# Seven front steps of the next image, dealt out ahead of the first slot

## The chip, the cores and the metric

The kernel runs on one core of a Trainium2 chip. The metric is the device time of one execution in microseconds. The median of three runs before the change is 5431.17 us (5421.16 to 5444.6). Beside them there is one execution under the hardware profiler, which took 4810.47 us; every duration in this document is from that execution unless it says otherwise, and its trace counts time from its first instruction.

## What is computed

There are 8 images of 256 channels and 64 x 64 pixels. Each goes through two residual layers, all in float32:

```python
x = x + L0(gn(x))   # 3x3 neighbourhood attention with 4 heads, mixed with
                    # convolution kernels generated per pixel, then a projection
x = x + L1(gn(x))   # modulated deformable 3x3 convolution

# gn: normalization over 32 groups of 8 channels
# L1: om = conv3x3(x, w_off) + b_off       27 channels: 9 x (dy, dx) and 9 masks
#     v[c,k,h,w] = bilinear sample of x at (h,w) + tap k + offset, times sigmoid(mask)
#     out = einsum('bckhw,ock->bohw', v, w)
```

The sampled positions depend on the data, so that layer 1 fetches rows of a table in memory by computed indices.

## The kernel before

**Two streams of work.** For each image there is a *front* and there are *slots*. The front is everything up to the sampling table: layer 0, the second normalization, the table, the offsets and the positions. It is written as a generator (`fronts`, L803, made of `attention`, L586, and `prepare`, L669) that yields 144 times an image; the piece between two yields is a *step*. The slots are the deformable convolution: an image has 8 chunks of 8 rows (512 pixels) and 9 taps, so 72 slots (`SLOTS`, L47). `STEPS` (L53) is 2 x 72 = 144, one step for each half of a slot.

**A slot** has four blocks of 128 pixels. Each block is fetched by one indirect gather on GpSimd (`gather`, L814), which brings four corner rows of 256 floats a pixel into one of 10 buffers of the tag g; ScalarE scales the first corner (`scale`, L828), VectorE adds the other three for two blocks at a time, six instructions (`sum_corners`, L839, L844), and with that the gather buffers are free again. TensorE transposes the four blocks (`transposes`, L858, tile pt), ScalarE copies the result (tile vt, L868), and in the next slot TensorE multiplies it by the tap's weights in two halves m = 0, 1 (`product`, L871, tile po, L890), accumulating over the nine taps. Gathers run up to 18 blocks ahead of the slot, scalings 8, sums 6 (`ahead`, L848).

**The order is written out by hand.** Inside `tc.manual_schedule` (L917) TensorE, ScalarE, VectorE and GpSimd execute in the order in which the code issues. First comes the whole front of image 0, 144 steps. Then ten gathers are issued (L927), and in a loop over i = 0, 2, 4 the first scalings, the first sums and further gathers (L929 to L939). Then the slots run: after each half slot the front is moved on until it has reached

```python
goal = h * STEPS + min(h, STEPS) * STEPS_AHEAD
```

where h counts half slots and `STEPS_AHEAD` is 12. So during image 0's 144 half slots the generator makes 156 steps, and it stays 12 steps ahead of the half slots from then on. In images 1 and later there is one step a half slot.

**The steps that the change touches** are the first of the next image's front: `means` (L184: a small TensorE product gn, L187, and four small VectorE operations, L189 to L193), `ready` (L195: a product gv, L198, a square root on ScalarE with its table load, L200, a reciprocal, L201), `normed` (L233: VectorE writes the first chunk's normalized rows into the tile xn, L248 and L253), a step that is empty in the first chunk, `q` (L299: tile psq, L304, copied by ScalarE, L312), and `k` for its two halves (L345, L331: tile psk, L336, copied by ScalarE, L349). Behind them come the two steps `products` (L361, tile qk, L375, masked by VectorE, L383), `logits` (L389), `generated` with the first part of the softmax (L405, L441), `v`, and so on. Steps 126 to 143 of a front (`prepare`) also issue the table writes (L690) and the loads of the image after (L91) on the SP queue.

Of the kernel before, what the change touches and what calls it, by code (L numbers as in the profile page):

```python
# [51 lines left out]
LEAD = SCALE_AHEAD + GATHERS  # L52
STEPS = 2 * SLOTS  # L53
STEPS_AHEAD = 12


@with_exitstack
def preact_kernel(ctx: ExitStack, tc: tile.TileContext, a: dict, out: bass.AP):
# [95 lines left out]
    for i in range(min(2, B)):  # L154
# [3 lines left out]
        for o in range(H * WP, ENTRIES, P):  # L158
            n = min(P, ENTRIES - o)
# [44 lines left out]
    def folded():  # L204

        ps = psum_a("eff")[:, : NT * HEADS * KK].rearrange(
            "p (c h k) -> p c h k", c=NT, h=HEADS
        )
        for ct in range(NT):
            for h in range(HEADS):  # L210
                for i in range(2):
                    nc.tensor.matmul(
                        ps[:, ct, h, :],
                        w_qkv[h // 2][:, 2 * (h % 2) + i, ct * P : (ct + 1) * P],
                        w_kgT[:, 2 * h + i, :],
                        start=(i == 0),
                        stop=(i == 1),
                    )
        return ps

    def fold(ps):

        for ct in range(NT):
            nc.vector.tensor_scalar(
                w_effT[:, ct, 0 : HEADS * KK],
                ps[:, ct].rearrange("p h k -> p (h k)"),
                alpha,
                None,
                ALU.mult,
            )  # L230
        nc.vector.tensor_scalar(bkg, bkg, alpha, None, ALU.mult)
# [48 lines left out]
    def first_stats(b, c):  # L280
        if c == 0:
            stats0[b] = p2.tile([P, NT, NC, 6], F32, tag="stats0", name=f"stats0_{b}")
        for ct in range(NT):
            nc.vector.bn_stats(
                stats0[b][:, ct, c, :], image[:, ct, c * N : (c + 1) * N]
            )
        if c == NC - 1:
            norm0[b] = Norm(stats0[b], f"0_{b}")
# [514 lines left out]
    def fronts():  # L803
        for b in range(B):
            gn = None
            for got in attention(b):
                gn = got
                yield
            yield from prepare(b, gn)
# [4 lines left out]
    def gather(i):  # L814
        if i >= B * BLOCKS:
            return
        b, n = divmod(i, BLOCKS)
        c, k, j = n // NB // KK, n // NB % KK, n % NB
        g = gp.tile([P, 4 * C], F32, tag="g", name=f"g_{i}")
        nc.gpsimd.indirect_dma_start(  # L820
            out=g,
            out_offset=None,
            in_=tables[b % 2],
            in_offset=bass.IndirectOffsetOnAxis(ap=found[b, c][0][:, j, k : k + 1], axis=1),
        )
        rows[i] = g

    def scale(i):  # L828

        if i >= B * BLOCKS:  # L830
            return
        b, n = divmod(i, BLOCKS)
        c, k, j = n // NB // KK, n // NB % KK, n % NB
        s = gp.tile([P, C], F32, tag="s", name=f"s_{i}", bufs=NB + SUM_AHEAD)
        g, w = rows.pop(i), found[b, c][1][:, j, k]
        nc.scalar.activation(s, g[:, 0:C], AF.Copy, scale=w[:, 0:1])  # L836
        sums[i] = s, g, w

    def sum_corners(i):  # L839

        work = [sums[n] for n in (i, i + 1) if n in sums]
        for q in range(1, 4):
            for s, g, w in work:
                nc.vector.scalar_tensor_tensor(  # L844
                    s, g[:, q * C : (q + 1) * C], w[:, q : q + 1], s, ALU.mult, ALU.add
                )

    def ahead(i):  # L848

        scale(i + SCALE_AHEAD)  # L850
        scale(i + SCALE_AHEAD + 1)
        sum_corners(i + SUM_AHEAD)
        gather(i + LEAD)
        gather(i + LEAD + 1)
# [3 lines left out]
    def transposes(b, n):  # L858
        c, k = divmod(n, KK)
        u = f"{b}_{c}_{k}"  # L860
        pt = [ps_t.tile([P, NB, P], F32, tag="t", name=f"pt_{u}_{ct}") for ct in range(NT)]
        for j in range(NB):
            s = sums.pop(b * BLOCKS + NB * n + j)[0]
            for ct in range(NT):
                nc.tensor.transpose(pt[ct][:, j, :], s[:, ct * P : (ct + 1) * P], ident)  # L865
        v = p2.tile([P, NT, N], F32, tag="vt", name=f"vt_{u}")
        for ct in range(NT):
            nc.scalar.copy(v[:, ct, :], pt[ct].rearrange("p b n -> p (b n)"))  # L868
        state["v", n] = v

    def product(b, n, m):  # L871

        c, k = divmod(n, KK)
        if k == KK // 2 and m == 0:
            r = p1.tile([P, NT, N], F32, tag="r", name=f"r_{b}_{c}")
            if b + 1 < B:
                nc.sync.dma_start(r, kept[b % 2][:, :, c * N : (c + 1) * N])
            state["r"] = r
        if k == 0 and m == 0:

            if b + 1 == B and c % 2:
                state["po"] = [psum_a(f"po_{b}_{c}_{i}") for i in range(NT)]
            else:
                po = ps_o.tile([P, NT, 512], F32, tag="o", name=f"po_{b}_{c}")
                state["po"] = [po[:, i, :] for i in range(NT)]
        po, v = state["po"], state["v", n]
        if m == NT - 1:
            del state["v", n]
        for ct in range(NT):
            nc.tensor.matmul(  # L890
                po[m],
                w_conv[:, ct, k, m * P : (m + 1) * P],
                v[:, ct, :],
                start=(k == 0 and ct == 0),
                stop=(k == KK - 1 and ct == NT - 1),
            )

    def finished(b, c, m):
        if m == 0:
            state["y"] = p1.tile([P, NT, N], F32, tag="y", name=f"y_{b}_{c}")  # L900
        nc.scalar.copy(state["y"][:, m], state["po"][m])  # L901

    def stored(b, c, m=slice(0, NT)):
        r, y = state["r"][:, m], state["y"][:, m]
        x1 = r if b + 1 < B else image[:, m, c * N : (c + 1) * N]
        nc.vector.tensor_add(r, y, x1)
        nc.sync.dma_start(
            out[b].rearrange("(t p) l -> p t l", p=P)[:, m, c * N : (c + 1) * N], r
        )
# [7 lines left out]
    with tc.manual_schedule(engines=ordered):  # L917
        ps = folded()
        for c in (0, 2, 1, 4, 3, 6, 5, 7):
            first_stats(0, c)  # L920
        fold(ps)
        steps = fronts()
        done = 0
        while done < STEPS:
            next(steps, None)
            done += 1
        for i in range(GATHERS):  # L927
            gather(i)
        for i in range(0, SUM_AHEAD, 2):  # L929
            if i == 0:  # L930
                scale(0)
                scale(1)
            scale(i + 2)
            scale(i + 3)
            sum_corners(i)
            gather(i + GATHERS)
            gather(i + GATHERS + 1)
        gather(SUM_AHEAD + GATHERS)
        gather(SUM_AHEAD + GATHERS + 1)  # L939
        last = None  # L940
        for n in range(B * SLOTS + 1):
            late, last = last, None
            if n > 0 and n % KK == 0:
                last = divmod(n // KK - 1, NC)
            for m in range(NT):
                if n < B * SLOTS:
                    if m == 0:
                        transposes(*divmod(n, SLOTS))
                    if not last:
                        ahead(NB * n + 2 * m)  # L950
                if late and m == 0:
                    stored(*late)
                if n > 0:
                    product(*divmod(n - 1, SLOTS), m)
                if last:

                    finished(*last, m)
                    ahead(NB * n + 2 * m)
                    if n == B * SLOTS:
                        stored(*last, slice(m, m + 1))  # L960

                h = NT * n + m + 1
                goal = h * STEPS + min(h, STEPS) * STEPS_AHEAD
                while (done - STEPS) * STEPS < goal:
                    next(steps, None)
                    done += 1

# [78 lines left out]
```

## Time and profile before

| | |
|---|---|
| median of the three runs | 5431.17 us |
| the profiled execution | 4810.47 us |
| its span, first to last instruction | 4808.7 us |
| mean granted TensorE clock | 0.985 |
| busy share: TensorE, VectorE, GpSimd, ScalarE | 96%, 87%, 61%, 51% |
| front of image 0 alone | 0 to about 312 us |
| first gather issued | 312.66 us |
| first deformable product (po) | 333.62 us |
| first finished chunk stored | 409.72 us |
| from there to the same chunk of image 1 | 594.4 us |
| the same stretch in the five images after | 576.4 to 579.7 us |

A row of the profile is a group of instructions: the line of the kernel, the engine, the operation, and out<-in by the names of tiles. PE is TensorE's matmul and PEld its weight load, DVE is VectorE, ACT ScalarE, POOL GpSimd, SP the queue that issues plain DMAs. In answers in order of time the first two numbers are the start and the duration in microseconds, and a bracket at the end holds the idle time before and what ended it. The profile counts a float32 matmul as two instructions, so that the four matmuls of q are eight rows.

### The profile page before, as it was taken

To read this page: it belongs to the slowest core of one execution; us is meant where nothing else is said; L and a number is where in the kernel's file an instruction comes from. 1 tells how busy PE (TensorE), PEld (TensorE's weight loads), DVE (VectorE), ACT (ScalarE), POOL (GpSimd) and SP (SyncE) were. 2 spreads that over 40 slices of the span, in tenths; PEclk is the share of its full clock that TensorE was granted. 3 is DMA by queue.
4 is the path that set the end of the run, shared out by engine and by line. 5 is a ranking of instruction groups with operands and counts; after the bars stand their busy time and mean duration, and the time that the engine had idled before them with its cause. 6 is when DMAs were issued, how large, how long until landed. Compare 5 with 4: busy or idle time off the path is not lost.

```text
span 4808.7 us, 80080 instructions
## 1 busy us (share of the span) xinstructions
PE 4597.8 (96%) x26848; PEld 2612.5 (54%) x26848; DVE 4185.7 (87%) x10066; ACT 2464.7 (51%) x5312; POOL 2954.5 (61%) x2310
## 2 busy tenths in 40 slices
PE   8979999999999999999999999999999999998888
PEld 5635555555545555455555555555555555544343
DVE  5568988899988998988988899899998899988887
ACT  3335555455555555555554555555555555554554
POOL 0026666566656666466674666756666666657776
PEclk9989999999999999999999999999999999999999
DMA  2077878888898878988889888888788888888998
GB/s 98 23 243 280 285 281 329 292 306 305 295 338 308 296 287 288 354 292 294 309 298 332 303 293 295 317 330 293 288 299 335 297 293 302 285 307 336 365 370 319
DMA packets 472649, 1414.24 MB, mean 294 GB/s; under 512 B 46814, under 2 KB 114654, under 8 KB 472108
## 3 DMA queue, kind: packets, MB, share of 16 engines
q0 software_dynamic: 331776, 1208.11, 68.6%
q1 hardware_dynamic: 138444, 197.65, 11.5%
q8 instruction: 211, 3.46, 0.3%
q10 hardware_dynamic: 2016, 3.38, 0.2%
q14 instruction: 202, 1.65, 0.1%
HBM read 1276.02 MB, written 132.94 MB: 293 GB/s over the span
## 4 chain that ended last, share of the span: by engine, by line
PE 73%; DVE 12%; DMA 10%; issue 3%; ACT 2%; POOL 0%; DVEq 0%; POOLq 0%; ACTq 0%
PE po L890 29%; DMA g<-table,idx 9%; PE pt L865 8%; DVE s L844 7%; PE om L701 6%; PE psk L336 4%; PE psq L304 4%; PE psv L336 4%; PE proj L561 3%; PE av L549 3%; PE qk L375 2%; PE vk L531 2%; PE ptab L681 2%; PE gt L427 1%; PE gen L409 1%
## 5 line engine op out<-in xcount | busy, mean ns | idle before, releaser
L820 POOL DMA_INDIRECT g<-table,idx x2304 | 2952.0, 1281 | 1832.8 <-DVE s L844 784.7
L844 DVE SCALAR_TENSOR_TENSOR s<-g,wt,s 128x256 f32<-128x256 f32 x6912 | 2814.0, 477 | 207.2 <-ACT s L836 197.7
L890 PE MATMUL po<-vt,w_conv 128*128 128x512 f32 x4608 | 2203.6, 604 | 31.4 <-ACT y L901 31.4
L836 ACT ACTIVATE s<-g,wt 128x256 f32<-128x256 f32 x2304 | 1090.3, 511 | 613.5 <-DMA g<-table,idx 514.0
L890 PEld LDWEIGHTS po<-vt,w_conv 128*128 128x128 f32 x4608 | 816.9, 193 | 762.1 <-issue 703.8
L868 ACT COPY vt<-pt 128x512 f32<-128x512 f32 x1152 | 616.7, 588 | 350.8 <-PE pt L865 349.4
L865 PE MATMUL pt<-ident,s 128*128 128x128 f32 x4608 | 661.2, 282 | 71.0 <-DVE s L844 52.0
L865 PEld LDWEIGHTS pt<-ident,s 128*128 128x128 f32 x4608 | 530.6, 143 | 324.8 <-issue 135.5
L701 PE MATMUL om<-xn,w_off 128*32 128x512 f32 x2304 | 288.1, 596 | 0.0
L383 DVE TENSOR_TENSOR qk<-qk,near_k 128x400 f32<-128x400 f32 x256 | 134.0, 568 | 161.9 <-PE qk L375 158.7
L336 PE MATMUL psv<-xn,w_qkvT 128*128 128x264 f32 (+1 forms) x1088 | 258.9, 382 | 0.0
L336 PE MATMUL psk<-xn,w_qkvT 128*128 128x264 f32 (+1 forms) x1088 | 254.6, 379 | 0.0
L336 PEld LDWEIGHTS psv<-xn,w_qkvT 128*128 128x128 f32 x1088 | 201.2, 191 | 85.2 <-issue 49.5
L336 PEld LDWEIGHTS psk<-xn,w_qkvT 128*128 128x128 f32 x1088 | 201.7, 190 | 83.0 <-issue 38.8
L304 PE MATMUL psq<-xn,w_qkvT 128*128 128x512 f32 x512 | 236.2, 603 | 10.1 <-DVE wk L516 8.6
L561 PE MATMUL proj<-acc,w_projT 128*128 128x512 f32 x512 | 240.7, 593 | 0.7 <-ACT acc L556 0.7
L710 ACT ACTIVATE om<-om,b_off 128x512 f32<-128x512 f32 x64 | 44.1, 688 | 270.3 <-PE om L701 270.3
L701 PEld LDWEIGHTS om<-xn,w_off 128*32 128x32 f32 x2304 | 74.2, 109 | 199.2 <-issue 161.0
L349 ACT COPY k<-psk 128x264 f32<-128x264 f32 (+1 forms) x272 | 100.2, 372 | 157.0 <-PE psk L336 155.4
L358 ACT COPY v<-psv 128x320 f32<-128x320 f32 (+1 forms) x272 | 106.2, 414 | 138.6 <-PE psv L336 138.0
L253 DVE TENSOR_SCALAR xn<-x,gn 128x576 f32<-128x576 f32 (+2 forms) x256 | 177.2, 734 | 0.0
L304 PEld LDWEIGHTS psq<-xn,w_qkvT 128*128 128x128 f32 x512 | 95.2, 190 | 143.3 <-issue 91.1
(94 smaller groups left out, 3430.3 us busy)
## 6 DMA issues: line engine op xcount, KB each, us to landing
table<-ts SPq DMA_DIRECT2D x384, 176.0 KB
g<-table,idx POOLq DMA_INDIRECT x2304
out_dram<-r SPq DMA_DIRECT2D x63, 512.0 KB
x<-in_x_dram SPq DMA_DIRECT2D x61, 512.0 KB
x<-x SPq DMA_DIRECT2D x56, 512.0 KB
r<-x SPq DMA_DIRECT2D x56, 512.0 KB
w_conv<-in_w_conv_dram SPq DMA_DIRECT2D x1, 2304.0 KB
x<-in_x_dram ACTq DMA_DIRECT2D x3, 512.0 KB
```

Of the source, the lines that this page charges most:

```text
L253: nc.vector.tensor_scalar(xn[:, ct, o : o + hi - lo, 1 : W + 1], xt[:, ct, lo * W : hi * W].rearrange("p (r w) -> p r w", w=W), gn[:, 0, c ...
L304: nc.tensor.matmul(ps, w_qkvT[:, ct, m * P : (m + 1) * P], window(self.xn, ct, 4), start=(ct == 0), stop=(ct == NT - 1),)
L336: nc.tensor.matmul(ps[:, : (hi - lo) * WP], w_qkvT[:, ct, o : o + P], self.xn[:, ct, lo:hi, :], start=(ct == 0), stop=(ct == NT - 1),)
L549: nc.tensor.matmul(av[64 * h : 64 * h + 64, g, t * T * T : (t + 1) * T * T], self.vk[:, t, o : o + 64], self.wk[2 * g + h][:, i * n + t * ...
L561: nc.tensor.matmul(ps, w_projT[:, ct, m * P : (m + 1) * P], self.acc[:, ct].rearrange("p (t y x) -> p y t x", y=T, x=T), start=(ct == 0), ...
L701: nc.tensor.matmul(ps[32 * g : 32 * g + 32, :], w_off[:, ct, k, :], window(xn, ct, k), start=(n < 4), stop=(n >= KK * NT - 4),)
L820: nc.gpsimd.indirect_dma_start(out=g, out_offset=None, in_=tables[b % 2], in_offset=bass.IndirectOffsetOnAxis(ap=found[b, c][0][:, j, k : ...
L836: nc.scalar.activation(s, g[:, 0:C], AF.Copy, scale=w[:, 0:1])
L844: nc.vector.scalar_tensor_tensor(s, g[:, q * C : (q + 1) * C], w[:, q : q + 1], s, ALU.mult, ALU.add)
L865: nc.tensor.transpose(pt[ct][:, j, :], s[:, ct * P : (ct + 1) * P], ident)
L868: nc.scalar.copy(v[:, ct, :], pt[ct].rearrange("p b n -> p (b n)"))
L890: nc.tensor.matmul(po[m], w_conv[:, ct, k, m * P : (m + 1) * P], v[:, ct, :], start=(k == 0 and ct == 0), stop=(k == KK - 1 and ct == NT - 1),
```

## The change

After image 0's 144 front steps three more steps are made (means, ready, normed of image 1) before the first gather is issued. In the loop that issues the first scalings and sums, two steps are made behind the first pair of sums (the empty one and q) and one behind each of the two others (the halves of k). `done` starts at 151, and the remaining five steps ahead are spread over the 144 half slots of image 0. From the end of image 0's slots on, the order is that of before.

```diff
 STEPS_AHEAD = 12
+STEPS_FIRST = 7
...
         steps = fronts()
-        done = 0
-        while done < STEPS:
+        for n in range(STEPS):
             next(steps, None)
-            done += 1
+
+        for n in range(STEPS_FIRST - 4):
+            next(steps, None)
         for i in range(GATHERS):
             gather(i)
         for i in range(0, SUM_AHEAD, 2):
...
             sum_corners(i)
             gather(i + GATHERS)
             gather(i + GATHERS + 1)
+            for n in range(2 if i == 0 else 1):
+                next(steps, None)
+        done = STEPS + STEPS_FIRST
...
                 h = NT * n + m + 1
-                goal = h * STEPS + min(h, STEPS) * STEPS_AHEAD
-                while (done - STEPS) * STEPS < goal:
+                goal = h * STEPS + min(h, STEPS) * (STEPS_AHEAD - STEPS_FIRST)
+                while (done - STEPS - STEPS_FIRST) * STEPS < goal:
                     next(steps, None)
                     done += 1
```

On TensorE this puts gn, gv, the products of q and of k in front of slot 0's transposes, where before they stood between slots 0 and 3. On VectorE the four small operations, the reciprocal and the normalizing stand in front of the first sums. On ScalarE the table load and the square root stand in front of the first scaling, the copies of q between the scalings of blocks 3 and 4, and the copies of k between those of 5 and 6 and behind that of 7.

## Prediction

> **What bounds the kernel now.** I read the page's forty slices first, then the waits of TensorE, then a table by stage around the first slot, and last the instructions there in order of time. The slices say that TensorE is the busy engine from the third slice on, and that the one hole is early:
>
> ```profile
> PE   8979999999999999999999999999999999998888
> PEclk9989999999999999999999999999999999999999
> DMA  2077878888898878988889888888788888888998
> ```
>
> Each slice is 120 us. The weak ones, the third of both upper rows, hold the change from the first image's front to its first slot. The waits between 290 and 420 us say what TensorE lacked there:
>
> ```profile
> PE pt L865 <- DVE s L844: 12.5, 2, 10.9
> PE gv L198 <- DVE gnd L193: 4.9, 1, 4.9
> ACT s L836 <- DMA g<-table,idx: 21.3, 18, 4.9
> ```
>
> Columns: total us, times, longest. TensorE waits for the corner sums of the first samples, these for ScalarE's scaling, and that for the gathers. In stretches (wall us, then busy us of PE, PEld, DVE, ACT, POOL, then granted clock, DMA share, GB/s):
>
> ```profile
> 304.00:312.00 8.00, 6.77 (x56) 3.14 (x54) 3.83 (x15) 2.64 (x6) 0.00 (x0) 1.00 0.53 170
> 312.00:316.00 4.00, 0.00 (x0) 0.00 (x0) 3.65 (x15) 0.00 (x0) 2.73 (x3) 0.74 0.37 124
> 316.00:320.00 4.00, 0.00 (x0) 0.00 (x0) 1.04 (x4) 0.51 (x1) 3.07 (x4) 0.50 0.81 247
> 332.00:336.00 4.00, 4.00 (x12) 2.63 (x12) 3.29 (x10) 2.94 (x7) 3.09 (x4) 0.50 1.03 407
> 336.00:340.00 4.00, 4.00 (x8) 1.62 (x7) 4.00 (x11) 1.51 (x3) 2.19 (x3) 0.77 1.02 408
> 344.00:409.00 65.00, 61.76 (x397) 37.49 (x395) 52.37 (x124) 34.85 (x79) 44.22 (x34) 1.00 0.71 253
> ```
>
> So there is a gap of some 22 us (311.6 to 333.6) with 5 us of TensorE work in it, and behind it the clock is half until about 337.7. From 344 on TensorE is 95% busy, VectorE 81%: TensorE binds. The rows that the change touches:
>
> ```profile
> 322.55 1.12 PE L865 MATMUL pt<-ident,s 128*128 128x128 f32 x4 [10.93 <-DVE s L844]
> 331.46 0.56 PE L198 MATMUL gv<-gnd,gmat 128*128 128x2 f32 x2 [4.93 <-DVE gnd L193]
> 333.62 5.70 PE L890 MATMUL po<-vt,w_conv 128*128 128x512 f32 x8
> 339.15 3.61 PE L304 MATMUL psq<-xn,w_qkvT 128*128 128x512 f32 x8
> 331.12 1.28 ACT L200 ACT_TABLE_LOAD   x1
> 335.30 1.51 DVE L253 TENSOR_SCALAR xn<-x,gn 128x576 f32<-128x576 f32 x2
> ```
>
> **What moves, and its price.** The seven steps are the next image's means, its deviation, its first normalized rows, an empty step, q, and both halves of k. They hold no DMA; nothing of them goes through SP or POOL, and the ten first gathers keep their order. None is removed: afterwards 149 steps instead of 156 are dealt to the first image's 144 half slots, and from its end on the order is as before. Only that image can gain or lose. Its later steps come up to seven half slots earlier, fading to none; those that store, load or write tables go through SP earlier by as much, each an issue of 0.4 to 0.6 us on a queue with time between its issues, so I cost them at nothing (if a table write met the full DMA of 770 to 861 us, at most its own few us).
>
> TensorE: q 3.44, k 2.68 and 1.78 us by the chain of waits at full clock, together 7.9, and two tiny products (0.42 and 0.56). VectorE: four small operations over 0.74 us (330.57 to 331.31), a reciprocal 0.17, zeroing and normalizing 1.6; 2.5 in all. ScalarE: square root 0.26 with its table load, two q copies of 0.59, k copies of 2 x 0.27 and 4 x 0.38: 3.2 without the load. Today all this stands inside slots 0 to 3, where TensorE's part is on the path.
>
> **The gap walked through.** The statistics are ready at 316.55. Each hop of the chain gn, four small operations, gv, square root, reciprocal is taken from today's rows (0.15 us from VectorE to TensorE, 0.39 from TensorE to the others): gn ends 317.1, gv 318.95, the reciprocal 319.8, the normalized rows 321.55. The first scaling now waits behind the square root in ScalarE's queue until 319.6 (it ran at 316.82), but the second could not run before 320.28 anyway, so the pair is done at 320.8. The first six sums start at 321.55 behind the normalizing and end at 324.0 instead of 322.9. The buffer that this frees is asked for by the eleventh gather, which POOL's own pace of 1.25 us brings at 325.47: no cost.
>
> q starts at 321.7, cold: a pass of 128x512 takes 0.853 us (5.70 us row, weight loads spaced 0.34 + 0.52), warm 0.43. Both ends: 6.8 us if it stays cold throughout, 3.4 if warm. Today the first full-sized products start at 333.6 and the clock is released some 4.1 us later; I take that row, so five passes are cold and q ends at 327.2. The Trainium skill (TensorE: Matmul & The Clock Gate, Part 1) puts it as a window: about 3.4 us idle halves the clock, about 3.4 us of steady work frees it. It speaks against filling a gap with matmuls that all run at half speed. With 3.4 us q would end at 326.8. The granted clock of 0.50 agrees that the array is cold here, but today's four cold passes of the convolution (some 2 us lost) disappear in exchange, since q and k warm the array first; so the rule costs nothing on balance, by either number.
>
> k follows without a hole: first half to 329.9, second to 331.7. ScalarE copies q at 325.5 and 327.6, so the scalings of blocks 4 and 5 come at 328.2 to 329.2 (today 324.2 and 325.5), those of 6 and 7 behind the k copies, done at 331.6. That is the new wait: queued behind these copies are the scalings, and VectorE's sums wait for those. Sums of blocks 6 and 7 end near 334.0 (today 330.6). Slot 0's transposes run at 331.7 to 332.6 instead of 322.5; they cost nothing, because slot 0's product waits behind slot 1's transposes. Steps 8 and 9 (the qk products, 0.9 each) then fill TensorE to 334.4, slot 1's transposes end at 335.3, and the first convolution product starts at 335.3 against 333.6.
>
> Beyond that VectorE is short: qk masks 2.1 and the logits 3.0 us now come before the sums that slot 2 needs, so its transposes start near 344, about 1.4 us after TensorE is free; I find one more such wait, 1.8 us, ahead of slot 4, behind the softmax twists (2.8 us). Counting on with 0.87 us for a slot's transposes and 3.44 for its products, TensorE has finished slot 4's product and the next chunk's q near 372.5. Today the same step ends with slot 7's product at 393.7. The three products between (5, 6 and 7 with their transposes) are 3 x 4.31 = 12.9 us, so the new kernel stands there at 385.4: **8 us ahead**.
>
> A second way to the same number: from the first stored chunk to that of the next image took 594.4 us in image 0 (409.72 to 1004.17), and 576.4 to 579.7 in the five after it. That stretch has 63 slots of image 0 and 9 of the next, so 10.5 of the 12 extra steps: 16.8 us over the mean of 577.6, or 1.6 a step. Seven steps less are 11.2, minus the 1.7 of the late first product: 9.5, and less the 3 us of waits for VectorE 6. I take 8.
>
> The profiled execution took 4810.5 us (span 4808.7); the median of the runs shown is 5431.2, 12.9% more, and no row tells why. I take the gap to stretch likewise: 8 x 1.129 = 9 us, 5422. All runs shown lie within 23 us, and 0.5% of the time, 27 us, is about what a measurement can tell from no change; this gain is below that.
>
> **The rivals.**
> *Absorbed.* The gathers begin at the same 312.66, and DMA shares run at 1.03 around 332 and 0.98 at 770 to 861 (the table writes). If a timed run is held by gathers rather than by TensorE, work taken off TensorE brings nothing: 5431. For it speaks that scaling waits 21.3 us for gathers in the window; against it that TensorE is 98 to 100% busy in each 100 us from 400 to 700. Chance 0.13.
> *All of image 0's excess goes.* The first chunk took 76.1 us from the first product (333.6 to 409.7) against 68.3 in the next image, 7.8 more; with the 16.8 that is 24.6, times 1.129 28: 5403, just over 0.5% faster. It needs the remaining five steps to be free as well, in waits that the profile doesn't show. Chance 0.17.
> *VectorE stays behind.* Slots start with fewer sums in hand than today. VectorE is 91% busy between 400 and 500 us, so the debt may not be repaid: a wait of some 1.5 us ahead of each slot's transposes, over three chunks (27 slots), is 40 us, minus the 11.2 taken off: +29, times 1.129 +33: 5464. It decides from the seventh such slot on (7 x 1.6 = 11.2). Against it: before, VectorE idled 1.2 to 3.7 us at a time between 344 and 355, which is what repays the debt. Chance 0.14.
>
> **How the numbers follow.** Likeliest, 0.56: 5422, with its own range of 5408 to 5438 (cold or warm q, 3 us; no or twice the VectorE waits, 3 us; the runs' own spread, some 10 us). Range for 8 in 10: 5400 to 5450, which takes in the absorbed case, the edge of the second rival and half of the way to the third. Faster by over 0.5% is the second rival, 0.17; slower the third, 0.14; within, 0.69.
>
> **What would show it.** Right: q and k rows of image 1 between 321 and 332 us, the first passes at 0.85; the first product near 335; the wait of pt for the sums no longer 10.9 us but two or three of 1 to 2; the first stored chunk about 8 us earlier; later images unchanged at 577. Wrong: waits of pt for s spread over the first chunks (VectorE), longer waits of the scalings for gathers with TensorE idle (absorbed), or later images whose time changed, which nothing here foresees.

## The result and the profile after

| | before | after |
|---|---|---|
| median | 5431.17 us (5421.16 to 5455.17, 9 runs) | 5441.59 us (5398.45 to 5461.17, 9 runs) |
| ratio after / before | | 1.0011, 95% interval 0.9991 to 1.0031 |
| profiled execution, span | 4810.47, 4808.7 us | 5435.43, 5433.7 us |

No difference that this comparison can tell. Two later comparisons of the same two kernels gave 1.0012 (0.9995 to 1.0029) and 1.0020 (1.0006 to 1.0034). Weighting the three by the inverse square of their half widths gives 1.0015 with a half width of 0.001: the changed kernel is some 8 us slower, where 9 us less was forecast. Neither of the first two alone tells that from no change.

One thing has to be known before any number here is compared. The runs went to several chips, and **the chips differ by 13%, each of them in every execution**: on one (the quick chip below) every execution of every kernel took 4791 to 4833 us, on the others 5393 to 5508. The profiled execution shown with the kernel before was of the first kind, the timed runs beside it of the second. So the profile of after can't be laid beside that of before to tell what the change did; each is compared with a profile of its own kind below.

The slices of after, for those shown of before:

```profile
PE   8988999999999999999999999999999999997777
PEclk9999999999999999999999999999999999998888
DMA  2177679777797677877788777877679776788876
```

The slices are longer now (136 us), and the weak third one is still weak. In the same columns as before (wall, busy us of PE, PEld, DVE, ACT, POOL, clock, DMA share, GB/s), the stretches around the first slot:

```profile
316.00:320.00 4.00, 1.52 (x4) 1.00 (x4) 2.75 (x9) 1.22 (x4) 2.86 (x4) 0.50 0.98 303
332.00:336.00 4.00, 1.50 (x9) 0.65 (x10) 0.00 (x0) 1.01 (x2) 3.09 (x4) 1.00 0.95 366
336.00:340.00 4.00, 2.41 (x21) 1.91 (x21) 1.57 (x4) 0.00 (x0) 0.49 (x1) 0.54 1.03 418
```

The gap of 316 to 320 has TensorE work now, as meant. But from 332 to 340, where before was full (4.00 and 4.00), TensorE is busy for 3.9 of 8 us and VectorE for 1.6 and ScalarE for 1.0. The waits of TensorE from 290 to 420 us:

```profile
PE qk L377 <- issue: 7.1, 13, 1.2
PE gn L189 <- DVE mv L184: 5.3, 1, 5.3
```

The waits of pt for the sums (12.5 us) are gone. In their place stand 13 short ones of qk for "issue", in which TensorE waited for nothing that the profile shows. In order of time:

```profile
319.11 5.46 PE L306 MATMUL psq<-xn,w_qkvT 128*128 128x512 f32 x8 [1.55 <-issue]
324.41 4.62 PE L338 MATMUL psk<-xn,w_qkvT 128*128 128x132 f32 x24
328.87 1.04 PE L867 MATMUL pt<-ident,s 128*128 128x128 f32 x8
329.83 1.08 PE L377 MATMUL qk<-k,q 64*64 64x100 f32 x36
331.20 0.37 PE L377 MATMUL qk<-k,q 64*64 64x100 f32 x2 [0.28 <-issue]
332.62 0.33 PE L377 MATMUL qk<-k,q 64*64 64x100 f32 x3 [1.05 <-issue]
333.34 0.24 PE L377 MATMUL qk<-k,q 64*64 64x100 f32 x1 [0.39 <-issue]
...
338.32 0.95 PE L377 MATMUL qk<-k,q 64*64 64x100 f32 x13 [0.23 <-issue]
339.21 1.97 PE L867 MATMUL pt<-ident,s 128*128 128x128 f32 x8
340.97 2.99 PE L892 MATMUL po<-vt,w_conv 128*128 128x512 f32 x4
```

The first 36 of 64 qk rows take 1.08 us, the other 28 take 8 us: they come in ones, twos and threes, and the starts lie 0.71 us or twice that apart. The first product waits for their end.

### The profile page after: what moved, and what is told of

Same layout as the page of the kernel before. It is cut to its first block, busy times and chain, and to the rows that moved or that the text cites. A ratio compares the mean times of both kernels' runs of the same rounds, so it can differ in the third digit from the quotient of the medians.

```text
span 5433.7 us, 80082 instructions
## 1 busy us (share of the span) xinstructions
PE 4892.5 (90%) x26848; PEld 2766.8 (51%) x26848; DVE 4187.6 (77%) x10066; ACT 2454.4 (45%) x5312; POOL 2984.2 (55%) x2310
## 5 line engine op out<-in xcount | busy, mean ns | idle before, releaser
L892 PE MATMUL po<-vt,w_conv 128*128 128x512 f32 x4608 | 2308.4, 629 | 34.0 <-ACT y L903 14.0
L838 ACT ACTIVATE s<-g,wt 128x256 f32<-128x256 f32 x2304 | 1063.8, 510 | 458.2 <-DMA g<-table,idx 400.7
L892 PEld LDWEIGHTS po<-vt,w_conv 128*128 128x128 f32 x4608 | 853.0, 201 | 810.5 <-issue 761.4
L377 PE MATMUL qk<-k,q 64*64 64x100 f32 x4096 | 224.6, 267 | 200.8 <-issue 191.1
L377 PEld LDWEIGHTS qk<-k,q 64*64 64x64 f32 x4096 | 143.3, 138 | 336.3 <-issue 298.3
L306 PE MATMUL psq<-xn,w_qkvT 128*128 128x512 f32 x512 | 239.5, 610 | 23.1 <-DVE wk L518 20.0
L551 PE MATMUL av<-wk,vk 100*64 100x64 f32 x4096 | 200.5, 258 | 33.8 <-issue 32.3
L551 PEld LDWEIGHTS av<-wk,vk 100*64 100x64 f32 x4096 | 173.7, 168 | 109.3 <-issue 89.9
L558 ACT COPY acc<-av 128x512 f32<-128x512 f32 x128 | 75.1, 587 | 306.5 <-PE av L551 231.7
L538 ACT COPY vk<-vk 100x512 f32<-100x512 f32 x256 | 138.2, 590 | 154.4 <-PE vk L533 145.7
```

Source lines behind the costliest of these rows:

```text
L306: nc.tensor.matmul(ps, w_qkvT[:, ct, m * P : (m + 1) * P], window(self.xn, ct, 4), start=(ct == 0), stop=(ct == NT - 1),)
L377: nc.tensor.matmul(both[h][64 * t : 64 * t + 64, n : n + NK], self.qt[r, ct, o * T * T : (o + 1) * T * T], kt[r, ct, :, T * o : T * o + KT ...
L551: nc.tensor.matmul(av[64 * h : 64 * h + 64, g, t * T * T : (t + 1) * T * T], self.vk[:, t, o : o + 64], self.wk[2 * g + h][:, i * n + t * ...
L892: nc.tensor.matmul(po[m], w_conv[:, ct, k, m * P : (m + 1) * P], v[:, ct, :], start=(k == 0 and ct == 0), stop=(k == KK - 1 and ct == NT - 1),
```

## The experiments

Marks below are us after the start of the last group of omt products (four, the last of the offsets) of image 0's front (310.54 in the profile of before), since the fronts differ by a few us from execution to execution.

### Both kernels on the quick chip

The two kernels as they are, a profile of each, on the chip where the kernel before took 4816.5 us (35 runs, 4804.68 to 4830.69).

Before:

> The kernel of before once more, to have its profile beside that of the changed kernel under like conditions (the first profile of before was 12.9% shorter than the runs, that of after was not). Theory 1 (the timed executions of both kernels lose time in stretches in which TensorE issues the small qk and av products slowly, and the first profile of before happened not to): span near 5430 us, granted clock near 0.94, some 300 us of PEld qk waiting for issue, and the first stored chunk at about 425 plus the 8 us that were forecast, so 433. Rival (the slow issue came with the change): span near 4810 us and almost no such wait.

After:

> The changed kernel once more: whether its profile repeats. Theory 1: 5430 to 5450 us, first product near 341 us, first stored chunk near 425. Rival (two states that any execution may fall in): now and then 4800 us, with the first product near 334.

4830.46 us before, 4823.97 after, both within the spread of before alone, so the totals tell nothing and the traces have to. Both expectations of about 5430 us were missed because the executions fell on the quick chip; neither trace has the slow issue, so they don't decide between the theories on it. From image 0's front to the first stored chunk of image 1, the kernel before in one row of the stretches (columns as above):

```profile
313.00:1009.00 696.00, 660.22 (x3906) 382.32 (x3907) 613.71 (x1480) 361.93 (x786) 449.87 (x343) 0.98 0.83 296
```

and the changed kernel:

```profile
313.00:1000.00 687.00, 660.49 (x3906) 380.56 (x3907) 613.92 (x1480) 360.50 (x787) 449.16 (x343) 0.99 0.84 300
```

The same 3906 matmul rows, the busy time of TensorE and VectorE the same within 0.3 us and of the others within 2 us, and 9 us less wall: what is saved in these two traces is TensorE's idle time and nothing else. By the marks the ninth chunk is stored at 686.8 us, against 693.6 and 696.4 in the two profiles of before: 6.8 to 9.6 us. The gap itself, changed kernel:

```profile
323.63 5.78 PE L306 MATMUL psq<-xn,w_qkvT 128*128 128x512 f32 x8 [1.55 <-DVE xn L255]
329.25 4.62 PE L338 MATMUL psk<-xn,w_qkvT 128*128 128x132 f32 x24
333.71 1.04 PE L867 MATMUL pt<-ident,s 128*128 128x128 f32 x8
334.67 1.63 PE L377 MATMUL qk<-k,q 64*64 64x100 f32 x64
336.24 1.09 PE L867 MATMUL pt<-ident,s 128*128 128x128 f32 x8
337.17 1.88 PE L892 MATMUL po<-vt,w_conv 128*128 128x512 f32 x4
```

Here the 64 qk rows take 1.63 us in one piece, and the first product starts 23.6 us after the mark's zero. TensorE's waits from 316 to 420 us, before:

```profile
PE pt L865 <- DVE s L844: 12.1, 2, 10.5
PE gv L198 <- DVE gnd L193: 5.0, 1, 5.0
```

and after:

```profile
PE gn L189 <- DVE mv L184: 5.4, 1, 5.4
PE qk L377 <- ACT k L351: 2.5, 1, 2.5
...
PE pt L867 <- DVE s L846: 0.9, 1, 0.9
```

### Three steps, and nine, on the same chip

*Three*: only means, ready and normed come ahead of the gathers; this was meant to give TensorE nothing large in the gap. *Nine*: both qk steps come ahead as well.

```diff
# three
-STEPS_FIRST = 7
+STEPS_FIRST = 3
-        for n in range(STEPS_FIRST - 4):
+        for n in range(STEPS_FIRST):
-            for n in range(2 if i == 0 else 1):
-                next(steps, None)
# nine
-STEPS_FIRST = 7
+STEPS_FIRST = 9
-        for n in range(STEPS_FIRST - 4):
+        for n in range(3):
-            for n in range(2 if i == 0 else 1):
+            for n in range(2 if i == 0 else 1 if i == 2 else 3):
```

Three:

> Only the three normalization steps (means, ready, normed) come ahead of the gathers; q and k stay in the slots. Theory of the forecast (what is moved into the gap is worth its TensorE time): 1 to 3 us of gain, since these steps hold 1 us of TensorE and one wait of 4.9 us that already lay in the gap; first product 2 to 4 us earlier than before's. Rival (the gain of the moved steps is eaten by slow issue of the first qk products, which seven steps push into the gap): three steps leave qk in the slots as before, and the first product comes near 331 us instead of 341.

Nine:

> Nine steps ahead: the two qk steps also stand before slot 0. Theory of the forecast: TensorE has 1.8 us less in the slots, total 10 us under before, first product no later than with seven. Rival (slow issue of qk): the first transposes wait behind qk, first product near 341 us as with seven or a few us later, total within 3 us of before.

Three: 4812.64 us (13 runs), ratio 0.9998 (0.9984 to 1.0012). Nine: 4810.43 (22 runs), ratio 0.9983 (0.9973 to 0.9994), 8 us faster by the ratio, 6 by the medians, where 10 had been expected. Their ninth chunks stand at 689.5 and 689.9. So bringing steps forward pays on this chip; for three steps the mark says 4 to 7 us and the totals say no difference, which is as far as one trace and an interval of 13 us go. The changed kernel with its seven steps was timed here only by its one profiled execution: its own gain there rests on the trace.

*Three* is not the contrast that it was meant to be. With the normalized rows ready, the steps dealt to the first two half slots are q and the first half of k, and these ran in the gap all the same, ahead of the first product:

```profile
330.57 6.15 PE L306 MATMUL psq<-xn,w_qkvT 128*128 128x512 f32 x8
336.56 2.84 PE L338 MATMUL psk<-xn,w_qkvT 128*128 128x132 f32 x16
```

So the two runs don't tell what q and k in the gap are worth from what the earlier normalization is worth. The first product came at 25.4 with three and 27.6 with nine, later than with before (22.7 and 23.1), where an earlier one, and one no later than with seven, had been expected. A later first product alone is thus no sign of a loss: it counts whatever ran ahead of it.

### The same on a slower chip, with the seven in one lump, and with twelve

Another chip; before takes 5431.88 us (51 runs). *Lump* makes all seven steps before the first gather. *Twelve* makes all twelve, the last six behind the third pair of sums.

```diff
# lump
-        for n in range(STEPS_FIRST - 4):
+        for n in range(STEPS_FIRST):
-            for n in range(2 if i == 0 else 1):
-                next(steps, None)
# twelve
-STEPS_FIRST = 7
+STEPS_FIRST = 12
-        for n in range(STEPS_FIRST - 4):
+        for n in range(3):
-            for n in range(2 if i == 0 else 1):
+            for n in range(2 if i == 0 else 1 if i == 2 else 6):
```

After:

> The changed kernel, timed again. Theory 1 (the forecast's mechanism: TensorE work moved into the gap is taken off the slots): where executions take about 4815 us, 6 to 10 us less than before, ratio 0.998 to 0.9985; in the trace, from the last omt product of image 0's front to the first stored chunk of image 1 some 687 us against 695. Theory 2 (nothing is gained, the sums and the gathers set the pace): ratio 1.000, the same stretch within 3 us of before. If executions take about 5430 us, theory 1 still has 8 us less in that stretch.

Before:

> Before, for the trace on this chip. Both theories: from the last omt product of image 0's front to the first stored chunk of image 1 694 to 697 us if executions take about 4815 us; about 785 us if they take 5430 (778.8 was seen for the changed kernel there; theory 1 adds 8).

Lump:

> All seven steps ahead of the first scalings and sums, not dealt out between them. ScalarE's scalings wait behind all copies of q and k, the first sums come some 9 us later, and the gathers wait for their buffers. Theory 1: first convolution product 31 to 33 us after the last omt product instead of 23.6, so 7 to 9 us of the gain gone, total within 2 us of before. Theory 2 (it does not matter where they stand, the slots catch up): like the changed kernel.

Twelve:

> All twelve steps ahead of the first slot (the two qk steps, the logits, gen and the first part of v behind the third pair of sums). Theory 1: TensorE's moved work grows from 7.9 to 13.5 us, of which the gap still hides what fits before the sums of slot 1 are ready; 9 to 12 us under before, at most 3 better than seven. Theory 2: 0. The rival that VectorE stays behind: first product 29 us or later after the last omt product, and total no better than before.

| | median us | ratio (95%) |
|---|---|---|
| before, its profiled execution | 5427.12 | |
| after | 5438.20 | 1.0012 (0.9995 to 1.0029) |
| lump | 5448.72 | 1.0032 (1.0020 to 1.0045) |
| twelve | 5429.56 | 0.9998 (0.9982 to 1.0014) |

None gains here, whatever the number of steps, and the lump is slower than before. It puts q and k ahead of the first gathers and so the sums behind them, and the waits of pt that the change removes are back in its trace:

```profile
332.68 0.83 PE L867 MATMUL pt<-ident,s 128*128 128x128 f32 x4 [2.98 <-DVE s L846]
335.06 1.11 PE L867 MATMUL pt<-ident,s 128*128 128x128 f32 x4 [1.54 <-DVE s L846]
```

That is 4.5 us. The lump's median is 10.5 us behind the changed kernel's, but the two intervals overlap, and its first product (30.9) and ninth chunk (785.5) stand within 1.5 us of the changed kernel's, so the trace shows no more than the waits. In *twelve* the first product came at 37.4, the first chunk at 122.4 and the ninth at 772.6. A first product after 29 and no gain were to be the signs of VectorE staying behind, but TensorE's waits for the sums are 1.7 us there up to 435 us. What the chips do differently stands in the waits of the whole execution. The changed kernel on this chip:

```profile
PE qk L377 <- issue: 184.1, 262, 2.7
PE pt L867 <- ACT vt L870: 95.1, 24, 10.0
```

and on the quick one, where this is TensorE's longest entry and qk never waits for issue:

```profile
PE pt L867 <- DVE s L846: 39.2, 61, 7.1
```

The marks of stored chunks (us after the zero):

| kernel, chip | first po | chunk 1 | 3 | 5 | 7 | 9 |
|---|---|---|---|---|---|---|
| before (profile shown), quick kind | 23.1 | 99.2 | 242.8 | 389.7 | 550.7 | 693.6 |
| before, quick | 22.7 | 98.2 | 243.5 | 390.3 | 551.6 | 696.4 |
| after, quick | 23.6 | 100.8 | 240.4 | 383.9 | 547.0 | 686.8 |
| before, slower | 22.9 | 109.1 | 272.1 | 447.4 | 613.3 | 768.5 |
| after, same slower chip | 31.6 | 117.8 | 288.0 | 453.5 | 628.6 | 784.2 |
| after (first profile), slower kind | 31.8 | 116.1 | 284.3 | 450.1 | 624.8 | 778.8 |

On the slower chip the changed kernel is 8.7 us late already at the first product and the first chunk, and 10 to 16 us at the ninth. Adding up the wall time of all bursts of the small products qk and av (first start to last end) from the zero to the ninth chunk gives some 40 us for either kernel on the quick chip, and on the slower one 91 (before) and 108 (after): about 17 us more slow issue in image 0 of the changed kernel, which is more than the gain. For before 785 us had been expected at the ninth chunk, and it stood at 768.5. The later images are alike in both kernels, 576 to 582 us on the quick chip and 647 to 659 on the slower. How far one trace can be trusted shows behind the ninth chunk, where the order of the two kernels is the same: there the changed kernel's profile is 14 us the shorter one (spans 5431.4 and 5425.3, less the marks and the zeros of 313.40 and 308.88). What repeats is the late first product, 31.6, 31.8 and 32.2 in three profiles of the changed kernel, where the same order has 23.6 on the quick chip.

### Is it the length of a run of small products?

In the slow bursts above, TensorE ran fast for the first tens of small matmul rows and then slowly. One theory: a long unbroken run of them is what falls behind. The changed kernel puts the two qk steps back to back (64 rows), where before a half of po stood between (32 and 32). *Split* is the changed kernel with the first half slots' steps held back so that a half of po stands between the two qk steps. *Spread* is the kernel before with a group of 32 av rows moved one step on, out of the step that holds 32 qk rows.

```diff
# split (changed kernel)
+                held = {1: 1, 2: 1, 3: 2, 4: 3, 5: 5, 6: 6}.get(h)
                 while (done - STEPS - STEPS_FIRST) * STEPS < goal:
+                    if held is not None and done - STEPS - STEPS_FIRST >= held:
+                        break
# spread (kernel before)
             a_.products(1)
-            if d:
-                d.weighted(0)
             yield None
             a_.logits()
             if d:
+                d.weighted(0)
```

Split:

> The changed kernel with its two first qk steps kept apart: the second is held back until half of a convolution product stands between them, and the steps after it catch up by the seventh half slot. Theory A (where executions take 5430 us, TensorE's small matmuls are supplied slowly once more than some 80 of them with as many weight loads follow each other; the change brought the first two qk steps together, 64 matmuls in 8.8 us instead of 2 x 0.93, and that took the gain away): the first product stands at 23 to 25 us after the last omt product instead of 31.6, both qk steps at 0.93, and the time is 8 us under the changed kernel's, so 5430 against before's 5432, or less. Where executions take 4815 us: like the changed kernel, within 3 us. Theory B (the slow supply depends on the traffic of the gathers, not on the run of small matmuls): qk stays slow, some 8 us, wherever it stands among the first gathers.

Spread:

> Before, with one step changed in every chunk: the first half of the attention product (32 av matmuls) goes from the step of the second qk products to the next one, so that nowhere 64 small matmuls stand together. Theory A: where executions take 5430 us, the bursts of 64 that took 4 to 12 us there and 2.0 where they take 4815 are gone, 56 of them: 250 to 500 us less, 4930 to 5180. Where executions take 4815: within 10 us of before. Theory B: no more than 30 us less.

Before took 5480.4 us (35 runs) on this chip. Split 5482.66, ratio 1.0002 (0.9985 to 1.0019); spread 5479.22, ratio 0.9996 (0.9977 to 1.0015). The theory falls: spread was to take 250 to 500 us less. In spread a single qk step of 32 rows, with half a slot's product ahead of it, still breaks up:

```profile
480.91 0.60 PE L375 MATMUL qk<-k,q 64*64 64x100 f32 x12
481.83 0.24 PE L375 MATMUL qk<-k,q 64*64 64x100 f32 x1 [0.32 <-issue]
482.55 0.40 PE L375 MATMUL qk<-k,q 64*64 64x100 f32 x3 [0.47 <-issue]
484.01 0.33 PE L375 MATMUL qk<-k,q 64*64 64x100 f32 x3 [1.05 <-issue]
```

And in split the first two qk steps take 1.61 and 0.93 us, but now the k copies of ScalarE ahead of them come late, so that the first po comes at 29.8 us and not at 23.6:

```profile
336.81 0.38 ACT L351 COPY k<-psk 128x264 f32<-128x264 f32 x1 [4.03 <-PE pt L867]
339.68 0.38 ACT L351 COPY k<-psk 128x264 f32<-128x264 f32 x1 [2.49 <-remote]
```

This looks like a stall that has moved to ScalarE. It has not. A copy waits for a semaphore, a counter that the engine before it raises, and the trace keeps the times of these updates. Both copies start 0.02 us after an update (336.79 and 339.66) of the one semaphore that only TensorE's matmuls raise, while the two groups of psk that they copy had ended at 332.06 and 332.95 by the trace. So TensorE's signals were 4.7 and 6.7 us late, and 2.87 us apart, four times 0.72. Since the ends of matmuls are modelled in these profiles, this does not tell whether the products themselves or only their signals were late. "remote" stands where no instruction was found to have ended shortly before the update: all 158 such waits of ScalarE and VectorE in the first profile of after, and all 157 in that of split, are for this semaphore of TensorE.

The other theory on record, that the traffic of the gathers makes the qk products slow wherever they stand among the first gathers, does not fit split's qk of 1.61 and 0.93 us either; what it says of late signals was not tested.

### Warming TensorE's clock in the gap

The changed kernel with five unread products put between the last offset product and the normalization steps; the rest as it is.

```diff
+        warm = psum_a("warm")
+        for n in range(5):
+            nc.tensor.matmul(
+                warm, w_qkvT[:, 0, 0:P], window(xn2[1], 0, 4), start=(n == 0), stop=(n == 4)
+            )
         for n in range(STEPS_FIRST - 4):
             next(steps, None)
```

After:

> The changed kernel as it is, timed once more. On a chip where the kernel before takes about 4815 us the theory (TensorE gets the 7 to 10 us that the first image's excess loses, and nothing takes them back) gives 4807, a ratio of 0.9980 to 0.9985, with the ninth chunk stored some 687 us after the last offset product of the first front (693.6 and 696.4 before). On a chip where it takes about 5430 us the theory of slow issue (the products issue slowly from the first chunk on, which takes the gain back) gives a ratio of about 1.001, the first deformable product 31 to 32 us after that point and the ninth chunk near 780. The rival, that the change is absorbed everywhere, gives 1.000 on either chip.

Warm:

> The changed kernel with five unread 128x512 products (4.3 us cold) put on TensorE between the last offset product and the three normalization steps, so that its clock may be released when q comes. The prediction's theory, that the cold clock costs nothing on balance, since slot 1's sums are last and not TensorE: q takes 3.6 to 4.9 us instead of 5.8, k ends up to 2 us earlier, the first deformable product comes within 1 us of the changed kernel's, and the total is within 3 us of it. The rival, that the cold products in the gap are paid for in full: first product 2 us earlier and total 2 us less on a 4815 us chip. If the clock counts only what runs without a pause, the five products end before q starts and nothing changes: q stays at 5.8.

A slower chip again (before 5472.58 us, 43 runs). After: 5478.63 us, ratio 1.0020 (1.0006 to 1.0034). Warm: 5483.59, ratio 1.0020 (1.0004 to 1.0037). The first interval leaves out 1.000, if narrowly: here the change costs time, and is not merely absorbed. A ratio of about 1.001, a first product at 31 to 32 and a ninth chunk near 780 had been expected of slow issue; 1.0020, 32.2 and 783.5 came. In warm:

```profile
315.72 4.55 PE L930 MATMUL warm<-xn,w_qkvT 128*128 128x512 f32 x10
321.20 0.35 PE L189 MATMUL gn<-mv,gmat 128*128 128x2 f32 x2 [0.93 <-DVE mv L184]
...
324.40 5.37 PE L306 MATMUL psq<-xn,w_qkvT 128*128 128x512 f32 x8 [1.55 <-DVE xn L250]
329.61 4.62 PE L338 MATMUL psk<-xn,w_qkvT 128*128 128x132 f32 x24
334.06 1.04 PE L867 MATMUL pt<-ident,s 128*128 128x128 f32 x8
341.55 2.94 PE L377 MATMUL qk<-k,q 64*64 64x100 f32 x64 [6.45 <-ACT k L351]
```

The five products ran warm (0.91 us each, clock 1.00 from 312 to 324), not cold as I had put it. But they end at 320.27, q starts at 324.40, and in the 4.1 us between stand only the two tiny products. Then q takes 5.37 us against 5.68 in after. The granted clock by stretches:

```profile
320.00:324.00 4.00, 0.99 (x5) 0.59 (x4) 2.52 (x10) 0.66 (x2) 3.08 (x4) 1.00 0.82 269
324.00:328.00 4.00, 3.60 (x6) 1.68 (x7) 3.80 (x9) 1.41 (x3) 3.08 (x4) 0.70 0.95 343
328.00:332.00 4.00, 4.00 (x18) 2.73 (x17) 3.24 (x8) 2.31 (x7) 3.08 (x4) 0.88 1.02 414
```

At half speed for 0.30 / 0.5 x 4 = 2.4 us of the second stretch and 1.0 of the third, the clock was half from about 325.6 to 329.0: it still was full when q began and fell while q ran, 5.3 us after the five products. This is nearly the third case of the expectation. So whether a warm q would bring the 2 us was not settled. The late signals of TensorE are here as well: qk runs in one piece, ScalarE's k copies come 6.4 us late ("remote", again TensorE's semaphore), and the first po comes at 31.3 us against 32.2 in after.

## Why the prediction was right and wrong

**The total: in range, by luck.** 5441.6 us lies within the 5400 to 5450 that were given, and a difference too small to tell was given 0.69. But it lies outside the likeliest case's own range (5408 to 5438), and what held it there is not in the forecast: a gain of 7 to 10 us that the quick chip's trace shows, and, if that gain is there on the slower chips too, some 16 us lost again; a stall of TensorE that the forecast did not know is the likely place.

**Where the gap is and what fills it: right.** On the quick chip the wait for the first sums went from 12.1 to 0.9 us and the one for the normalization chain from 5.0 to 0.9, and the wait for the statistics (gn, 5.4 us) came in front, where nothing else is to do.

**The walk through the gap: right within 1.2 us.** Counted from the zero, q was forecast at 11.2 and came at 10.05, 5.5 us long and measured 5.78 (five to six of eight passes cold); the first product was forecast at 24.8 and came at 23.6. For slots 2 and 4, 1.4 and 1.8 us of waiting for VectorE's sums were forecast; one wait of 0.9 came. "VectorE stays behind" did not happen on either kind of chip. Two slips of the working cost nothing: the cold row of 5.70 us holds about five cold passes ((5.70 - 3.44) / 0.42) and not the four set against them, and the five later images average 577.9 us and not 577.6.

**The cold clock costs nothing on balance: not settled.** In the one run that was to warm q, the clock fell while q ran.

**"8 us ahead": right in size at the end of image 0 on the quick chip, wrong in place.** I compared the same front step at two different slots (4 and 7) and took off three products, as if no step went with slots 5 to 7. Compared at the same slot, the changed kernel still makes 149/144 steps a half slot, and after 9 slots (18 half slots) it has been spared only 18 x 7/144 = 0.9 steps, 1.4 us at the 1.6 us a step of the second way, which the late first product takes back. The first chunk was 1.6 to 2.6 us later, where I had written "about 8 us earlier" as the sign of being right; the lead grew over the image (chunk 5: 5.8 to 6.4, chunk 9: 6.8 to 9.6). The second way, steps times 1.6 less the late product, has a mechanism that fits the growing lead: 9.5 forecast.

**"I take the gap to stretch likewise": the step that failed.** The 12.9% between the profiled execution and the timed runs was no stretch. It is the difference between two chips, and in image 0 most of it is one thing: bursts of small products that issue slowly. There they grew from 40 to 91 us in the kernel before, 51 of the 72 us by which that stretch is longer (768.5 against 696.4); in the whole execution, 337 of 597 us. A stretched gap would have given 9 us. Instead the qk products that the change brings forward met slow issue before the first product, and lost 8 us there, where before ran them fast:

```profile
352.24 0.93 PE L375 MATMUL qk<-k,q 64*64 64x100 f32 x32
355.02 0.94 PE L375 MATMUL qk<-k,q 64*64 64x100 f32 x32
```

That before is spared at this place does not hold for every execution: in spread, which has the same order up to here, the first qk step broke up too (29 rows in 1.18 us, then three single ones) and took 4.0 us. The total came out at 1.0015 instead of 0.9984: the sign was wrong on the chips that were timed. 5422 was forecast and 5441.6 came; against the before of the same comparison that is 10 us more instead of 9 less. That the stall ahead of the first product makes up this difference is likely, by the 8 us and by its return in three profiles, but no run takes the stall away and leaves the change: split and warm kept it in another form.

**The rivals.** *Absorbed* is the nearest by number on the slower chips, but not by its mechanism: the scalings' waits for gathers are shorter there (390 to 443 us in the whole execution against 550 on the quick chip), and TensorE waits more. *All of image 0's excess goes* fell: image 0 took 586.0 us on the quick chip, still above the 576 to 582 of the others, and twelve steps gained nothing in total where they ran.

**What stays open.** Why TensorE stalls on some chips. Shown: the stalls came in every profile from the slower chips, in none from the quick one, whatever the kernel; they come once or so in each attention chunk; the pieces and the late signals lie multiples of about 0.71 us apart; and they are TensorE's where ScalarE or VectorE stand still as well. Not shown: what it waits for. The packets of TensorE's own instruction queue (16 KB each) take about 1 us on both kinds of chip and don't land at the stalls.

One rival is untested: that the recording itself holds TensorE up on these chips. Their profiles have lost records: the first profile of after keeps 4214 of the 4785 semaphore updates that its TensorE instructions make, 8186 of 9684 of VectorE's and 4357 of 5229 of ScalarE's, and the others from slower chips lose about as many; the quick chip's profile of after keeps 4784, 9673 and 5228. The losses lie where the stalls do: of the updates of VectorE and ScalarE due within 5 us of the start of a stall (the first qk or av row that waits for "issue") some 55% are missing, of those due 5 to 20 us ahead of it some 3%. Whether the stalls cost the records, or the writing of records makes the stalls, this does not tell. The timed runs have a span and a granted clock each, so they too were recorded in some form, and part of the 13% could belong to the recording and not to the kernel.

That twelve lost nothing and seven some 8 us on the slower chips follows from where the stalls happen to fall, and this I only argue.

## What to carry to other kernels

Before a profiled time is scaled to a timed one, ask where the difference between them is: if the profile was taken under another condition, its gaps can be covered or replaced there, and multiplying a gain by the ratio means nothing. When work is moved ahead, compare the two kernels at the same slot, and count what each has still to do there; work that was dealt out evenly comes back as an even gain, not at once. A hole in a busy engine can be filled for what it is worth (9 us less idle time for 8 us of work on the quick chip), but moving a burst of many small instructions can also move the place where it stalls. When an engine seems to wait for nothing, look up which semaphore ended its wait and who raises it: here that put the stalls of three engines down to one.

## What the hardware showed beside this

- The same program took 4816.5 us on one chip and 5431.9, 5480.4 and 5472.6 on three others, with mean granted clocks of 0.982 to 0.989 on the first and 0.930 to 0.941 on the others. The lower clock follows at least in part from the stalls: the transposes behind a stall of 8 us take 1.97 us where they take 1.09 without one.
- On the slower chips 64 small matmul rows (64x100, float32) took 7 to 9.5 us where they broke up, instead of 1.6 to 1.8, in pieces 0.71 us or twice that apart. ScalarE's copies vt and VectorE's masks qk waited up to 10 us for late signals of TensorE, 69 times each in the first profile of after, with 64 attention chunks in all.
- Five warm full-sized products did not keep TensorE's clock over a pause of 4.1 us with 0.7 us of tiny products in it: it fell 5.3 us after them, in the middle of q, and four or five of q's eight passes ran at half speed ((5.37 - 3.44) / 0.42). The Trainium skill (TensorE: Matmul & The Clock Gate, Part 1) has about 3.4 us of idling for the same, which agrees if tiny products don't count; no run here tells whether they do.
